# Graph attention on 16 row groups: the first group computes h W before its attention

## The chip, the cores and the metric

The kernel runs on one core of one Trainium2 chip. The metric is the device time of one execution in microseconds. The engines are named as in the profile: PE (TensorE), DVE (VectorE), ACT (ScalarE), POOL (GpSimd) and SP (SyncE, which issues transfers).

## What is computed

The input x is 128 graphs of 64 nodes with 512 features, in float32. One adjacency matrix serves all graphs. The reference, cut to what matters:

```python
h = jnp.maximum(_layernorm(x), 0.0)
# first layer, 4 heads, W: [4, 512, 512], a: [4, 1024]
Wh = einsum('bnf,hfo->bhno', h, W)
f1 = einsum('bhno,ho->bhn', Wh, a[:, :O]);  f2 = einsum('bhno,ho->bhn', Wh, a[:, O:])
e = f1[:, :, :, None] + f2[:, :, None, :]
e = where(e > 0, e, 0.01 * e);  e = where(adj > 0, e, -1e9)
attn = softmax(e, axis=-1)
h1 = elu(einsum('bhnm,bhmo->bhno', attn, Wh))      # heads side by side: 2048 features
# second layer: the same with one head and W_out: [2048, 512], then elu -> out
y = maximum(out @ w1 + b1, 0) @ w2 + b2 + out
x + layernorm(y) * gamma + beta
```

## The kernel before

The 8192 rows are 64 tiles of 128 rows (two graphs each). Four tiles form a group, and there are 16 groups. A group passes through norm and relu (`norm1`), scores and softmax, attention of the first layer (`attend1`), the projection by the four W (`project1`), the second layer (`project2`, `stage_e`) and the feed-forward part. The stages of neighbouring groups are interleaved: a main list of steps feeds TensorE, and a list of side steps is dealt out between them. The order on each engine is fixed when the program is built.

Attention and projection commute, because attention mixes rows and W mixes columns. The kernel uses this twice. First, it computes z = attention times h and then z W (`attend1`, `project1`). Each product is done in Strassen's way: seven products of quarter blocks ("pieces", four matmuls of 256 columns each) instead of eight, with sums of blocks formed on other engines. `weight_sums` forms the sums of the weight blocks on GpSimd and stores them to memory (`tc`); `piece` fetches blocks as they are needed. Second, the scores f1 and f2 come from h (W a), so the kernel folds a into W once at the start: `wa` holds W a for the four heads, and `project_f` and `scores1` make the scores of a group from it. `R`, `L` and `U` are what `project_f` makes.

The fold at the start is made in two ways. `spread_a` copies a row of a to all partitions with a matmul (tile `pab`), and `fold_dve` multiplies W by it and sums along the row on VectorE (tile `jk`, heads 0, 1 and 3). `fold_pe` transposes W on TensorE (tile `pwt`) and multiplies it by a (tile `pwa`, head 2).

So for group 0 nothing dense can start until W a is folded, the scores are made, the softmax is done and its weights are transposed (`transpose_weights`, tile `s1pt`). After that `attend1` (tile `pz`) and `project1` (tile `g_a`) run, and in between the scores of group 1 are made as side steps. `project2` of group 0 (tile `g_b`) follows.

PSUM has six banks for products (`bank`, tag "mm") and two more for small tiles (`aux`). W is loaded by ScalarE's queue at the very start, W_out, w1 and w2 later by GpSimd's queue (`fetch`, `more_sums`).

Of the kernel before, what the change touches and what calls it, by code (L numbers as in the profile page):

```python
# [22 lines left out]
def gat_preln_kernel(  # L23
# [27 lines left out]

    nc = tc.nc
# [25 lines left out]
    def bank(name):  # L78
        return ps.tile([P, 2, T], FP, tag="mm", name=name)

    def aux(shape, name):
        return ps.tile(shape, FP, tag="aux", name=name, bufs=2)
# [15 lines left out]
    X[0] = load(0)  # L98
    aj = const.tile([P, N], mybir.dt.int32, name="aj")
    for b in range(NB):  # L100
        nc.sync.dma_start(out=aj[ts(b, N), :], in_=adj)
    ar = wk.tile([2 * H, O], FP, tag="elu", name="ar", bufs=3)
    nc.sync.dma_start(out=ar, in_=a_heads.rearrange("h (r p) -> (h r) p", p=O))
    for t in range(1, G):
        X[t] = load(t)
    ah = wk.tile([2 * H * KC, P], FP, tag="elu", name="ah", bufs=3)
    nc.sync.dma_start(out=ah, in_=a_heads.rearrange("h (r p) -> (h r) p", p=P))
# [34 lines left out]
    homes = ("h11", "h22", "h12", "wh2", "out", "wh2", "out", "wh2", "out", "out")  # L142
    stages = ("ot", "rt", "out", "hS", "ot", "rt", "ot", "rt", "ot", "rt")
    MT, TC = {}, {}
    DIRECT = {}

    def fetch(m):
        MT[m] = big.tile([P, KC, O], FP, tag=homes[m], name=f"pw{m}")
        queue = nc.scalar if m < H else nc.gpsimd
        queue.dma_start(out=MT[m], in_=mats[m].rearrange("(k p) o -> p k o", p=P))  # L150

    def spread_a(m):

        ab = []
        for c in range(2):
            pb = bank(f"pab{m}_{c}").rearrange("p a b -> p (a b)")
            r = 2 * m + c
            nc.tensor.matmul(
                pb, ident[0:2 * H, r:r + 1].to_broadcast([2 * H, P]), ar, start=True, stop=True
            )  # L160
            ab.append(pb)
        return ab

    def turn_a():

        rows = H * 2 * KC
        pt = aux([P, rows], "pah")
        nc.tensor.transpose(pt, ah, ident[0:rows, 0:rows])
        aT = wk.tile([P, H, 2, KC], FP, tag="s1", name="aT")
        nc.scalar.copy(aT.rearrange("p h c o -> p (h c o)"), pt)  # L170
        return aT

    def fold_dve(m, ab):

        for k in range(KC):
            for c in range(2):
                junk = wk.tile([P, O], FP, tag="t", name=f"jk{c}_{m}_{k}")
                nc.vector.scalar_tensor_tensor(
                    junk, MT[m][:, k, :], 1.0, ab[c], ALU.mult, ALU.mult,
                    accum_out=wa[:, k, c * H + m:c * H + m + 1],  # L180
                )

    def fold_pe(m, aT):

        pw = aux([P, KC, 2], "pwa")
        for k in range(KC):
            pt = bank(f"pwt{m}_{k}").rearrange("p a b -> p (a b)").rearrange("p (o q) -> p o q", o=KC)
            for o in range(KC):
                nc.tensor.transpose(pt[:, o, :], MT[m][:, k, ts(o, P)], ident)
            wT = wk.tile([P, KC, P], FP, tag="elu", name=f"wT{m}_{k}", bufs=3)  # L190
            nc.scalar.copy(wT, pt)
            for o in range(KC):
                nc.tensor.matmul(
                    pw[:, k, :], wT[:, o, :], aT[:, m, :, o],
                    start=(k == 0 and o == 0), stop=(o == KC - 1), skip_group_check=True,
                )
        nc.scalar.copy(wa[:, :, m:m + H + 1:H], pw)

    def weight_sums(m, after=None):

        w = MT.pop(m)
        b11, b12 = w[:, 0:2, 0:Q], w[:, 0:2, Q:O]
        b21, b22 = w[:, 2:4, 0:Q], w[:, 2:4, Q:O]
        tag = stages[m]
        if tag[1] == "t":
            s = [big.tile([P, 2, 2, Q], FP, tag=f"{tag}{i}", name=f"pt{m}_{i}") for i in range(2)]
        else:
            both = big.tile([P, 2, 2, 2, Q], FP, tag=tag, name=f"pt{m}")
            s = [both[:, 0], both[:, 1]]
        free = [nc.gpsimd.tensor_tensor(s[0][:, 0], b12, b11, ALU.subtract)]  # L210
        nc.gpsimd.tensor_tensor(s[0][:, 1], b22, s[0][:, 0], ALU.subtract)
        free.append(nc.gpsimd.tensor_tensor(s[1][:, 0], b22, b12, ALU.subtract))
        for ins in free if after is not None else ():
            tc.add_manual_dep(
                ins.ins, after.ins.name,
                mybir.DependencyInfo(mybir.DependencyClass.Sync, mybir.DependencyReason.DATA),
                reason="the sums come behind it",
            )
        nc.gpsimd.tensor_tensor(s[1][:, 1], b21, s[0][:, 1], ALU.subtract)
        TC[m] = [dram.tile([P, 2, 2, Q], FP, name=f"tc{m}_{i}") for i in range(2)]  # L220
        for i in range(2):
            nc.gpsimd.dma_start(out=TC[m][i], in_=s[i])
        if m < 2:
            for p, i in ((5, 0), (6, 1), (7, 2), (4, 3)):
                DIRECT[m, p] = s[i // 2][:, i % 2]

    def piece(m, p):

        if (m, p) in DIRECT:
            return DIRECT.pop((m, p))  # L230
        w = ring.tile([P, 2, Q], FP, tag="w", name=f"w{m}_{p}")
        if p in (1, 2, 3):
            r, c = {1: (0, 0), 2: (1, 0), 3: (1, 1)}[p]
            src = mats[m][r * Q:(r + 1) * Q, c * Q:(c + 1) * Q].rearrange("(k p) o -> p k o", p=P)
        else:
            i = {5: 0, 6: 1, 7: 2, 4: 3}[p]
            src = TC[m][i // 2][:, i % 2]
        nc.sync.dma_start(out=w, in_=src)
        return w
# [100 lines left out]
    def norm_stats(src, tag, t):  # L340
# [4 lines left out]
        if tag == "n1" and t >= 2 * G:  # L345
            tc.add_manual_dep(
                ins.ins, LAST["pe"].ins.name,
                mybir.DependencyInfo(mybir.DependencyClass.Sync, mybir.DependencyReason.DATA),
                reason="x may come late: not in front of what is urgent",
            )  # L350
# [8 lines left out]
    def norm1(t):  # L359
# [7 lines left out]
        if t % G >= 2:  # L367
            HNS[t] = big.tile([P, T], FP, tag="hns", name=f"hns{t}", bufs=2)
            nc.gpsimd.tensor_tensor(HNS[t], HN[t][:, 0:T], HN[t][:, T:2 * T], ALU.add)
# [12 lines left out]
    def project_f(g):  # L382
# [15 lines left out]
        eng = nc.vector if g == 0 else nc.gpsimd  # L398
        eng.tensor_tensor(
# [167 lines left out]
    def flat(ap):  # L567
        return ap.rearrange("p a b -> p (a b)")

# [3 lines left out]
    def z_sums(g, h):  # L573
        z = ZB[g]
        ZSUM[h] = new_sums(f"z{g}_{h}")
        eng = nc.vector if (g, h) == (0, 0) else nc.gpsimd
        sums(eng, z["S1"][:, h], z["11"][:, h], z["12"][:, h], z["22"][:, h], *ZSUM[h])

    def project1(g, h):
# [3 lines left out]
        first = (g, h) == (0, 0)  # L583
        if h == 0:
            for b in ("11", "12", "S1", "22"):
                tag = "hS" if b == "S1" else "h" + b
                H1[b] = big.tile([P, H, 2, T], FP, tag=tag, name=f"h{b}_{g}")
# [3 lines left out]
        def post(what, a, b=None, to=None):  # L591
# [13 lines left out]
            post, (1, 2, 6, 5, 7, 3, 4) if first else (1, 5, 6, 2, 3, 7, 4),  # L605
# [9 lines left out]
        ]  # L615

# [180 lines left out]
    masks()  # L797
    for t in range(G):
        norm1(t)
    ab = {m: spread_a(m) for m in (0, 1)}  # L800
    aT = turn_a()
    fold_dve(0, ab[0])
    fold_dve(1, ab[1])
    fold_pe(2, aT)
    for t in range(G):
        transpose_h(t)
    fold_dve(3, spread_a(3))
    for m in range(H):
        weight_sums(m, LAST["nb"])
    project_f(0)  # L810
    scores1(0)
    for p in range(2):
        attn_weights(p)
    softmax_end = LAST["A"]
    transpose_weights(0)
    attn = attend1(0)
    for fn in attn[:2]:
        fn()
    head0 = project1(0, 0)
    for fn in head0[:2]:  # L820
        fn()
    transpose_weights(1)
    for fn in attn[2:]:
        fn()
    z_sums(0, 0)
# [14 lines left out]
    def more_sums(m):  # L840
        fetch(m)
        weight_sums(m, softmax_end)

    for t in range(G, 2 * G):
        prefetch(t)
    for g in range(NG):
        if g >= 1:
            side = stage_e(g - 1)
        else:
            side = sum(stage_a(1), [])  # L850
            for i, m in ((5, 4), (9, 5), (12, 6), (17, 7)):
                side.insert(i, lambda m=m: more_sums(m))
        done, n = 0, 6 * H
        for i in range(n):
            if i % 6 == 0:
                steps = head0 if (g, i) == (0, 0) else project1(g, i // 6)
            if (g, i // 2) != (0, 0):
                steps[i % 6]()
            while done * n < (i + 1) * len(side):
                side[done]()  # L860
                done += 1
        flush_late()
# [16 lines left out]
        if g == 0:  # L879
# [4 lines left out]
            run(project2(g), first + early + norms + scores + turns + [  # L884
# [39 lines left out]
```

## Time and profile before

| | us |
|---|---|
| median of 3 runs | 2320.62 (2318.3 to 2320.84) |
| span of the profiled run | 2318.7 |
| TensorE busy | 2279.8 (98%) |
| VectorE busy | 1272.2 (55%) |
| GpSimd busy | 1029.9 (44%) |
| ScalarE busy | 905.5 (39%) |

A line of a timeline gives the start, the length, the engine, the line of the code, the operation, the output and input tiles, their shapes and how many records were merged, and in brackets the idle time before them with what ended it. Busy time of TensorE is not work at its peak, since matmuls are pipelined. The profile also gives the clock that TensorE was granted, as a share of the full one.

### The profile page before, as it was taken

The numbers are of one execution on the slowest core, as the hardware profiler recorded it, in microseconds if no ns is written. First come the engines' busy times: TensorE is split into PE (matmuls) and PEld (weight loads), VectorE is DVE, ScalarE is ACT, GpSimd is POOL, SyncE is SP. The second block draws the span as 40 slices with busy tenths as digits, with TensorE's granted clock in tenths as the row PEclk, the third lists the DMA queues.
The fourth block names the chain that finished last, engine by engine and source line by source line (L and its number), as shares of the span: only waits on it lengthen the run. The fifth ranks groups of instructions, "written<-read, shape, count | busy, mean of one in ns | idle before, by whom it ended". The sixth has DMA issues, their size and how long they took to land. (4 is left out here: it accounts for less than half of the span.)

```text
span 2318.7 us, 33446 instructions
## 1 busy us (share of the span) xinstructions
PE 2279.8 (98%) x11933; PEld 1922.7 (83%) x11933; DVE 1272.2 (55%) x2210; ACT 905.5 (39%) x1623; POOL 1029.9 (44%) x917
## 2 busy tenths in 40 slices
PE   6999999999999999999999999999999999999997
PEld 4878888888888888888888888888888888888885
DVE  6635465555646555465555646555464654744427
ACT  2534425153352534425254252533525244251512
POOL 6664544425344352444425444253443525533324
PEclk8999999999999999999999999999999999999999
DMA  8545464554545445454454545445453454635543
GB/s 296 174 171 195 133 183 135 157 161 133 183 135 176 131 147 178 133 182 132 151 171 133 182 135 162 150 140 182 132 179 131 147 180 128 182 119 168 163 146 104
DMA packets 259571, 366.40 MB, mean 158 GB/s; under 512 B 24232, under 2 KB 147144, under 8 KB 259408
## 3 DMA queue, kind: packets, MB, share of 16 engines
q1 hardware_dynamic: 252784, 343.31, 47.3%
q0 software_dynamic: 4512, 16.78, 2.0%
q10 hardware_dynamic: 2112, 4.19, 0.5%
q8 instruction: 96, 1.57, 0.3%
q14 instruction: 67, 0.55, 0.1%
HBM read 336.92 MB, written 27.26 MB: 157 GB/s over the span
## 5 line engine op out<-in xcount | busy, mean ns | idle before, releaser
L322 PE MATMUL g_b<-w,h 128*128 128x256 f32 x2560 | 592.5, 379 | 0.0
L322 PEld LDWEIGHTS g_b<-w,h 128*128 128x128 f32 x2560 | 481.4, 190 | 63.7 <-issue 0.9
L307 PE MATMUL g_a<-z,w 128*128 128x256 f32 x1520 | 360.9, 380 | 0.7 <-DVE g_a L597 0.7
L307 PE MATMUL g_a<-zs_z,w 128*128 128x256 f32 x1504 | 350.9, 381 | 0.0
L307 PEld LDWEIGHTS g_a<-zs_z,w 128*128 128x128 f32 x1504 | 282.0, 190 | 60.8 <-issue 24.3
L307 PEld LDWEIGHTS g_a<-z,w 128*128 128x128 f32 x1520 | 287.2, 190 | 45.0 <-DVE g_a L597 6.1
L601 POOL TENSOR_TENSOR hS<-hS,h 128x512 f32<-128x512 f32 x64 | 83.1, 1299 | 354.8 <-DVE hS L565 354.8
L322 PE MATMUL g_b<-w,hS 128*128 128x256 f32 x1024 | 238.5, 379 | 0.0
L563 ACT ACTIVATE exc<-g_a 128x512 f32<-128x512 f32 x256 | 152.1, 594 | 179.0 <-DVE g_a L597 106.7
L565 DVE SCALAR_TENSOR_TENSOR h<-exc,g_a 128x512 f32<-128x512 f32 x192 | 131.7, 686 | 157.3 <-ACT exc L564 156.2
L322 PEld LDWEIGHTS g_b<-w,hS 128*128 128x128 f32 x1024 | 192.1, 190 | 25.8 <-issue 1.0
L564 ACT ACTIVATE exc<-exc 128x512 f32<-128x512 f32 x256 | 161.5, 631 | 7.0
L631 POOL TENSOR_TENSOR h<-h,h 128x512 f32<-128x512 f32 x64 | 86.8, 1364 | 135.3 <-PE g_b L322 135.3
L631 POOL TENSOR_TENSOR h<-hS,h 128x512 f32<-128x512 f32 x64 | 81.2, 1270 | 142.5 <-PE g_b L322 142.5
L481 ACT COPY at<-s1pt 128x512 f32<-128x512 f32 x64 | 34.7, 588 | 279.8 <-PE s1pt L479 279.8
L332 POOL TENSOR_TENSOR zs_z<-zS,z 128x512 f32<-128x512 f32 x63 | 89.0, 1414 | 122.6 <-PE g_a L307 118.6
L773 POOL TENSOR_TENSOR xr<-xr,bs 128x512 f32<-128x512 f32 x64 | 96.1, 1502 | 72.6 <-DMA xr<-in_x_dram 58.4
L307 PE MATMUL g_c<-ot,w 128*128 128x256 f32 x512 | 122.8, 383 | 1.4 <-DVE ot L735 1.4
L322 PE MATMUL g_d<-w,rt 128*128 128x256 f32 x512 | 121.5, 380 | 2.2 <-DVE o L765 1.5
L307 PE MATMUL g_a<-zS,w 128*128 128x256 f32 x496 | 117.2, 379 | 0.0
L655 DVE SCALAR_TENSOR_TENSOR jf<-wh,ao 128x512 f32<-128x512 f32 x128 | 99.0, 811 | 31.8 <-ACT wh L637 31.6
L333 POOL TENSOR_TENSOR zs_z<-z,zs_z 128x512 f32<-128x512 f32 x63 | 85.1, 1351 | 61.8 <-PE g_a L307 39.1
(159 smaller groups left out, 3485.8 us busy)
## 6 DMA issues: line engine op xcount, KB each, us to landing
w<-tc SPq DMA_DIRECT2D x632, 256.0 KB, 2.7
w<-in_L_gnn_W_heads_dram SPq DMA_DIRECT2D x192, 256.0 KB, 3.0
w<-in_L_gnn_W_out_dram SPq DMA_DIRECT2D x192, 256.0 KB, 2.7
w<-in_L_gnn_w_dram SPq DMA_DIRECT2D x96, 256.0 KB, 2.7
x<-in_x_dram SPq DMA_DIRECT2D x64, 256.0 KB, 3.8
xr<-in_x_dram SPq DMA_DIRECT2D x128, 128.0 KB, 2.7
out_dram<-o SPq DMA_DIRECT2D x128, 128.0 KB, 2.4
tc<-pt POOLq DMA_DIRECT2D x20, 512.0 KB, 4.2
```

Source lines behind the costliest of these rows:

```text
L307: LAST["pe"] = nc.tensor.matmul(bk[:, o, :], w[:, k, ts(o, P)], a[:, k, :], start=start and o == 0 and k == 0, stop=k == 1, skip_group_che ...
L322: LAST["pe"] = nc.tensor.matmul(bk[:, j, :], a[:, k, ts(j, P)], w[:, k, :], start=start and k == 0 and j == 0, stop=i == len(ms) - 1 and k ...
L332: eng.tensor_tensor(s2, s1, a11, ALU.subtract)
L333: eng.tensor_tensor(s4, a12, s2, ALU.subtract)
L481: nc.scalar.copy(AT[t].rearrange("p b h n -> p (b h) n"), pt)
L563: nc.scalar.activation(ex, src, AF.Relu, scale=-1.0)
L564: nc.scalar.activation(ex, ex, AF.Exp, scale=-1.0)
L565: nc.vector.scalar_tensor_tensor(dst, ex, -1.0, src, ALU.add, ALU.max)
L601: nc.gpsimd.tensor_tensor(dst, dst, H1["22"][:, h], ALU.add)
L631: nc.gpsimd.tensor_tensor(dst[:, h], x0[:, h], x1[:, h], ALU.subtract)
L655: nc.vector.scalar_tensor_tensor(junk, WH2[g][:, j], 1.0, ao[:, c, :], ALU.mult, ALU.mult, accum_out=f[:, c, j:j + 1],)
L773: nc.gpsimd.tensor_tensor(xr, xr, bs, ALU.add)
```

## The change

Group 0 is taken out of the scheme of the others. It computes h W directly (`head_w`, tile `hw`, 16 products of four matmuls of 512 columns, without Strassen), which needs only h and W. The scores of group 0 are read off these products: VectorE multiplies each by a spread row of a and sums along the row (tile `jw`, results in `f_0`). `scores0` spreads f2 with a matmul (tiles `dg` and `pe0`) and makes the softmax for two tiles at a time. `attend0` then applies the attention to h W, head by head, with matmuls of 64 columns (tile `pu`), and ends with the elu. `project2` of group 0 follows as before.

The fold of W a is needed from group 1 on. It is now made on VectorE alone, for all four heads (`fold`), between the steps of group 0. `spread_a` keeps a copy of the spread rows in SBUF (`asb`). The norms and transposes of group 1 move to the start; its scores, softmax and turns go into `project2` of group 0 as side steps, ahead of all others. The parts of W_out are fetched behind given products of h W.

The diff, cut to its core:

```diff
-    def fold_pe(m, aT):
...
-    def fold_dve(m, ab):
+    def fold(m, ab):
-        for k in range(KC):
-            for c in range(2):
+        for c in range(2):
+            for k in range(KC):
                 junk = wk.tile([P, O], FP, tag="t", name=f"jk{c}_{m}_{k}")
                 nc.vector.scalar_tensor_tensor(
                     junk, MT[m][:, k, :], 1.0, ab[c], ALU.mult, ALU.mult,
                     accum_out=wa[:, k, c * H + m:c * H + m + 1],
                 )
...
+    def head_w(m, j, asb):
+        pb = flat(bank(f"hw{m}_{j}"))
+        for k in range(KC):
+            LAST["pe"] = LAST["hw", m, j] = nc.tensor.matmul(
+                pb, HT[j][:, k, :], MT[m][:, k, :], start=k == 0, stop=k == KC - 1
+            )
+        nc.scalar.copy(flat(HW[j][:, m]), pb)
+        for c in range(2):
+            junk = wk.tile([P, O], FP, tag="t", name=f"jw{c}_{m}_{j}")
+            nc.vector.scalar_tensor_tensor(
+                junk, pb, 1.0, asb[c], ALU.mult, ALU.mult, accum_out=f_0[:, c, j, m:m + 1]
+            )
+    def scores0(p):
...
+        nc.vector.tensor_tensor(
+            dg, eye[:, None, :].to_broadcast([P, 2 * H, N]),
+            f2[:, :, None].to_broadcast([P, 2 * H, N]), ALU.mult,
+        )
+        pe = aux([P, 2 * H, N], f"pe0_{p}")
+        nc.tensor.matmul(
+            flat(pe), blkones.rearrange("p b n -> p (b n)"), flat(dg), start=True, stop=True,
+        )
+        A1[p] = softmax(pe, f1, 2 * H, "s1", p)
+    def attend0(h, r):
+        banks = [flat(bank(f"pu{h}_{r}_{b}")).rearrange("p (c j n) -> p c j n", c=KC, j=2) for b in range(NB)]
+        for j in range(2):
+            for c in range(KC):
+                for b in range(NB):
+                    rows = slice(b * N, (b + 1) * N)
+                    hw = HW[2 * r + j][rows, h, c // 2, (c % 2) * P:(c % 2 + 1) * P]
+                    nc.tensor.matmul(
+                        banks[b][:, c, j, :], hw, AT[2 * r + j][rows, b, h, :],
+                        start=True, stop=True, skip_group_check=True,
+                    )
...
-    ab = {m: spread_a(m) for m in (0, 1)}
-    aT = turn_a()
-    fold_dve(0, ab[0])
-    fold_dve(1, ab[1])
-    fold_pe(2, aT)
-    for t in range(G):
-        transpose_h(t)
-    fold_dve(3, spread_a(3))
...
-    project_f(0)
-    scores1(0)
...
+    block(0, range(G))
+    fold(0, spread[0][0])
+    weight_sums(0, LAST["nb"])
+    block(1, range(G))
+    fold(1, spread[1][0])
+    weight_sums(1, LAST["nb"])
+    norms[0]()
+    block(2, (0, 1))
+    fold(2, spread[2][0])
+    weight_sums(2, LAST["nb"])
+    norms[1]()
+    block(3, (0, 1))
+    scores0(0)
+    fold(3, spread[3][0])
+    more_sums(4)
+    block(2, (2, 3))
+    more_sums(5)
+    weight_sums(3, LAST["hw", 3, 1])
+    block(3, (2, 3))
+    scores0(1)
+    for m in (6, 7):
+        more_sums(m)
+    transpose_weights(0)
+    new_h1(0)
+    for fn in scores[:2]:
+        fn()
+    for h in range(H):
+        attend0(h, 0)
+    transpose_weights(1)
+    for h in range(H):
+        attend0(h, 1)
+    side1 = scores[2:] + turns
...
-            run(project2(g), first + early + norms + scores + turns + [
+            run(project2(g), side1 + first + early + norms + scores + turns + [
```

## The prediction

> **What bounds the kernel now.** First the slices of the page. TensorE is busy throughout except at the start, so whatever this change can win lies in the first 58 us and whatever comes later is a sum of matmuls.
>
> ```profile
> PE   6999999999999999999999999999999999999997
> PEclk8999999999999999999999999999999999999999
> ```
>
> The next view is TensorE's timeline of the start (start us, length, count in records; a float32 matmul is two records).
>
> ```profile
> 8.19 7.16 PE L158 MATMUL pab<-ar,ident 8*128 8x512 f32 x8 [8.19 <-DMA ar<-in_L_gnn_a_heads_dram]
> ...
> 40.37 1.99 PE L413 MATMUL s1pe<-R,L 64*64 64x256 f32 x16 [2.82 <-DVE n1ve L354]
> 47.74 1.94 PE L479 MATMUL s1pt<-ident,s1A 128*128 128x128 f32 x8 [5.38 <-DVE s1A L442]
> 49.61 6.22 PE L539 MATMUL pz<-at,hn 64*128 64x256 f32 x32
> ```
>
> Until 49.6 us TensorE only prepares scores, and waits for the softmax. Later in the same timeline:
>
> ```profile
> 75.24 1.89 PE L307 MATMUL g_a<-z,w 128*128 128x256 f32 x8
> 76.97 1.89 PE L307 MATMUL g_a<-zS,pt 128*128 128x256 f32 x8
> ...
> 115.68 1.89 PE L322 MATMUL g_b<-w,h 128*128 128x256 f32 x8
> 118.29 1.99 PE L307 MATMUL g_a<-z,w 128*128 128x256 f32 x8 [0.72 <-DVE g_a L597]
> ```
>
> One piece (four matmuls of 256 columns) takes 76.97 - 75.24 = 1.73 us. The second layer of group 0 starts at 115.7; with the last g_a piece and the wait ahead of it behind it (0.72 + 1.83), its start counts as 118.2. What follows is the same work in both kernels, so I compare this milestone.
>
> TensorE's clock in 2 us stretches (stretch, length, busy and count, clock, DMA share, GB/s):
>
> ```profile
> 40.00:42.00 2.00, 1.63 (x16) 0.57 0.92 264
> 48.00:50.00 2.00, 2.00 (x9) 0.50 0.96 367
> 52.00:54.00 2.00, 2.00 (x13) 0.51 0.33 127
> 54.00:56.00 2.00, 2.00 (x17) 1.00 0.00 0
> ```
>
> The clock is half until 54.0, 4.4 us after the pz matmuls begin. It was half before as well: pab advances 0.85 us per record of 512 columns, against 0.216 for 256 columns later, and transposes take 3.68/16 = 0.23 us at 17.5 us against 0.11 later. The 1.00 that the view prints before 36.9 is therefore a missing record, not a fast clock. At 40.3 the clock fell to half (0.57 in the first row) after TensorE had stood idle since 37.6.
>
> Last, weight loads of two tiles in small stretches of that timeline:
>
> ```profile
> 120.22 0.19 PEld L539 LDWEIGHTS pz<-at,hn 64*128 64x128 f32 x2 [0.33 <-issue]
> 120.22 0.30 PEld L539 LDWEIGHTS pz<-at,hn 64*128 64x128 f32 x4 [0.33 <-issue]
> ```
>
> Two loads for the two row halves run side by side in 0.19 us, and the next pair follows 0.11 us later. So 64-row loads overlap in pairs.
>
> And what VectorE, GpSimd and the queues pay for the operations that the change moves or repeats: VectorE's timeline, the answers on s2dg and on the transfers.
>
> ```profile
> 14.43 0.68 DVE L178 SCALAR_TENSOR_TENSOR jk<-pw,pab 128x512 f32<-128x512 f32 x1
> ...
> 15.04 0.68 DVE L178 SCALAR_TENSOR_TENSOR jk<-pw,pab 128x512 f32<-128x512 f32 x1
> ```
>
> ```profile
> L664 DVE TENSOR_TENSOR s2dg<-eye,f x16: 415/889/892, 194.1 to 2254.2; 128x256 f32<-128x256 f32 x16
> ```
>
> ```profile
> pw<-in_L_gnn_W_out_dram POOLq DMA_DIRECT2D x4, 1024.0 KB, 7.7
> ```
>
> One fold step starts 0.61 us after the one before; the diagonal for a score spread has a fast and a slow form; a 1 MB part of W_out lands 7.7 us after its issue.
>
> **What the Trainium skill says.** "TensorE: Matmul & The Clock Gate", Part 1 (The HAM clock gate): the array runs at half clock until it has been busy for a window of about 3.4 us, and falls back after one idle window. The trace agrees with both directions (54.0 and 40.3). It adds a condition: 7 us of pab on 8 rows and 20 us of transposes and 2-column matmuls did not raise the clock, so thin work hardly counts. Same page, LDWEIGHTS: the load's time goes by columns, not rows, and Part 3 says loads overlap where row groups differ; the pairs above agree. Part 1 also has ScalarE and VectorE as strict FIFO queues; the trace has nothing against it, and I use it twice.
>
> **The change, part by part** (times from the start, on the new order of instructions on each engine).
>
> *Start of the dense work.* hn0 and hn1 end at 15.1 (ScalarE loads its table at 12.25 in both kernels), hn2 and hn3 at 17.1; then two copies of a (0.6 each) and hT0: h W starts at 18.9. All W are there in time (the third landed at 17.5). Removed: the fold on TensorE (about 13 us of records between 17.5 and 30.6), hidden or not.
>
> *h W.* 16 products of 4 matmuls of 512 columns: 64 x 0.864 = 55.3 us at full clock (Strassen's 28 pieces took 48.4). Half clock for the first 4.4 us costs 2.2. Three further spreads of a, 2 x 0.87 each: 5.2. Transposes and a wait for hT2: 1.3. With 18.9 that is 82.9, call it 83. Banks come back early (the spread of head 1 needs only the reading of the first product), so no block waits for the folds.
>
> *VectorE beside it.* Each head has 8 jw and 8 jk, 9.8 us, under the 15.5 us of TensorE, but the order is one queue: 8 jk come after the last jw of a block, then the statistics of group 1 (4 x 1), then two softmaxes (8 operations of 0.69, about 5.5). From the end of head 1's product (52 us) VectorE has no gap: 36 us of work, until 88. Two waits lengthen this. hn4 stands on ScalarE ahead of the copy of head 2's second product, and its scale comes from GpSimd, behind the fetch of W_out's second part (issued after 45, median landing 7.7 us) and its four sums (1.27 each) and stores: about 62 against 60.5, so jw, and everything queued on VectorE behind it, moves by some 2 us; pe0_0 holds TensorE for as long. hn6 and hn7 do the same to the copies of head 2's later tiles: under 1 us. So h W ends at about 85.5, and dg1 (a 512-wide product; 0.7 to 1.7 us, from s2dg's 0.415 to 0.89 at half that size) ends at about 91.
>
> *The new gap.* TensorE stands from 85.5 to 91, longer than the idle stretch that lowered the clock at 40.3. I take half clock from there. Then pe0_1 1.7, s1pt pairs 2 x 0.95, four transposes of group 1 each behind a copy: the attention runs free from about 99.
>
> *Attention per head.* 8 rounds of 16 matmuls of 64 columns, 32 records, 16 pairs of loads. The trace shows no 64-column matmul on 64 rows. Bound below by pairs: 16 x 0.107 = 1.7 us at full clock, 3.4 at half. Bound above without overlap between loads: twice that. ScalarE needs 4 x 0.6 = 2.4 a round in the first half, 1.8 after; VectorE 1.5 to 2.1. Streaming fills only half of each pair's time (64 columns at 0.216 per 256 are 0.054, of 0.107), so I expect this not to raise the clock, as the transposes did not. I take 3.7 us a round at half clock: 29.6. The transposes in the middle with their copy add 2.2. Ends at 99 - 0.6 + 29.6 + 2.2 = 130.
>
> *Second layer.* Its first 4.4 us at half clock: 2.2 lost. Milestone 132.2 against 118.2: +14.
>
> *Moved.* Folded scores of group 1 (pf, s1pe, 16 s1pt) leave project1 and go into project2: 1.1 + 1.1 + 1.75 = 4.0 us of TensorE that the milestone no longer holds. Each softmax there (5.5 us) is followed by its transposes after three to four pieces of 1.73; GpSimd has R behind the hS sums. I estimate 2 us of waits (0 to 6).
>
> *Same answer, nothing:* other homes for W, the earlier a, the shorter list of direct pieces, R of group 0: all beside TensorE's h W. Groups 1 to 15 are untouched.
>
> Sum: 2318.7 + 14 + 4 + 2 = 2338.7 of span; times are 1.9 above spans (2320.63 for 2318.7): **2340**.
>
> **Rivals.**
> A. The clock stays high, or comes back in the attention. Then ScalarE paces it: 4 x 2.4 + 4 x 1.8 and copies, 18 us; the chain before it shrinks by 4, and the 2.2 go. Milestone about 114 to 117; with 4 + 2 and the 1.9: 2322 to 2325. For it: pz on 64 rows did raise the clock. Against: pz streams without pause, and the gap comes first.
> B. Faster than before: A and no gap, since VectorE is quicker or waits overlap. Milestone 83 + 5 of scores + 18 = 106, give or take 2; with 4 + 1 and the 1.9: 2312 to 2315. For it: 30 us less idle start. Against: VectorE's 36 us, counted from a measured step.
> C. Loads do not overlap at 64 columns, or TensorE starts a load only after the previous stream: 5 to 7 us a round, 8 x 1.3 to 8 x 3.3 more: 2350 to 2366. For it: no row measures it; against: the pairs.
>
> **How the numbers follow.** Main case (half clock in the attention, 2326 to 2350 with the bounds of gap, dg and waits): 0.57. A: 0.18. B: 0.12. C: 0.13. Within 0.2% is 2316 to 2325.3: A, less its upper edge. Faster 0.12, same 0.17, slower 0.71. The range leaves out most of B and the upper end of C: 2317 to 2356.
>
> **What would show it.** In the profile after: hw records from about 19 us, clock 1.00 from about 23; h W ending at 83 to 86; a wait of pe0 on VectorE's dg of 4 to 6 us; clock 0.50 in the pu stage, pairs of pu every 0.22 us or so; g_b from 130. Wrong if pu runs at 1.00, if the gap is missing, or if g_b starts before 118.

## The result, and the profile after

The changed kernel takes 2352.08 us (median of 4 runs, 2350.49 to 2357.86), the kernel before 2320.3 in the same runs: a ratio of 1.0143, with a 95% interval of 1.0125 to 1.0161. It is slower, by 31.8 us. The profiled execution is the slowest of the four (2357.86, a span of 2355.8), so the trace holds some 6 us more than the median run; in which stage they lie is not known.

Two lines of the slices on the page: TensorE starts dense work sooner, and the clock has a dip in the second and third slice that before did not have.

```profile
PE   7899999999999999999999999999999999999997
PEclk9789999999999999999999999999999999999999
```

TensorE's timeline of the first group:

```profile
18.75 9.71 PE L592 MATMUL hw<-pw,hT 128*128 128x512 f32 x16 [2.19 <-ACT hT L351]
...
75.52 9.60 PE L592 MATMUL hw<-pw,hT 128*128 128x512 f32 x22
93.41 2.04 PE L611 MATMUL pe<-dg,blkones 128*128 128x512 f32 x2 [8.29 <-DVE dg L606]
95.25 2.11 PE L449 MATMUL s1pt<-ident,s1A 128*128 128x128 f32 x8
...
103.12 13.49 PE L624 MATMUL pu<-at,hw 64*128 64x64 f32 x122
116.54 1.97 PE L449 MATMUL s1pt<-ident,s1A 128*128 128x128 f32 x8
118.88 2.04 PE L624 MATMUL pu<-at,hwS 64*128 64x64 f32 x16 [0.38 <-ACT at L451]
...
132.80 3.78 PE L297 MATMUL g_b<-w,h 128*128 128x256 f32 x8
```

h W starts at 18.75. In before the attention (`pz`) starts at 49.61, so the new way starts 30.9 us sooner. The second layer, though, starts at 132.80 in place of 118.2. The 114 us between are 66.4 of h W (to 85.1), 8.3 of waiting for dg, 3.7 of scores and transposes (93.4 to 97.1) and 35.7 of attention. Before needs 68.6 us from 49.61 to 118.2. The attention of group 0 comes in eight rounds, one for each head and pair of tiles; a round is 16 matmuls of 64 columns, 32 records.

The clock in 2 us stretches (busy time and count, clock, DMA share, GB/s) shows where it falls:

```profile
88.00:90.00 2.00, 0.00 (x0) 0.70 0.97 307
90.00:92.00 2.00, 0.00 (x0) 0.50 0.95 301
```

It falls in the wait for dg, and stays at 0.50 until 136.6, through all of the attention. In the second layer and in the next projection come waits that before did not have:

```profile
150.07 1.89 PE L449 MATMUL s1pt<-ident,s1A 128*128 128x128 f32 x8 [2.10 <-DVE s1A L412]
...
186.82 2.30 PE L349 MATMUL pth<-ident,hn 128*128 128x128 f32 x8 [4.57 <-ACT hn L337]
...
239.70 3.78 PE L282 MATMUL g_a<-zs_z,w 128*128 128x256 f32 x8 [2.92 <-ACT t_a L248]
```

The first is for the softmax of group 1 (`s1A`), the second for the norms of group 2 (`hn`), the third for a copied sum in the projection (`t_a`). In each of the three the clock falls some 2.2 us after TensorE has stopped, and is at half from 150.2 to 153.7, 184.4 to 191.2 and 239 to 245.8. From the second layer of group 1 on (234.40 before, 271.58 after) the two kernels need the same: 2084.3 and 2084.2 us. So all of the loss lies ahead of that point, in three stages. The table has every kernel of this study (start of g_b of group 0, of g_a of group 1, of g_b of group 1, and the span, in us, of the profiled execution):

| kernel | g_b, group 0 | g_a, group 1 | g_b, group 1 | span |
|---|---|---|---|---|
| before | 115.7 (counts as 118.2) | 184.5 | 234.4 | 2318.7 |
| after | 132.8 | 215.5 | 271.6 | 2355.8 |
| e1 | 130.7 | 213.9 | 268.7 | 2352.3 |
| e2 | 135.4 | 221.4 | 276.1 | 2359.5 |
| e3 | 130.4 | 211.2 | 267.5 | 2351.5 |
| e4 | 132.9 | 215.7 | 271.9 | 2355.9 |
| e5 | 128.9 | 209.0 | 265.9 | 2349.1 |
| e6 | 132.9 | 210.0 | 263.3 | 2347.4 |
| e7 | 133.3 | 217.7 | 269.0 | 2352.1 |
| b1 | 128.6 | 204.2 | 257.4 | 2341.0 |
| b2 | 123.6 | 197.6 | 250.6 | 2334.3 |
| b3 | 124.1 | 203.3 | 254.6 | 2338.5 |
| f2 | 119.9 (counts as 122.5) | 188.7 | 238.7 | 2322.2 |
| f3 | 116.4 (counts as 118.9) | 185.8 | 235.8 | 2319.3 |

The first stage loses 14.6 us (132.8 - 118.2), the second 16.4 (82.7 against 68.8 - 2.5 for the late piece of g_a), the third 6.2 (56.1 against 49.9). Together 37.2, the difference of the two spans being 37.1. The first stage's loss is told by what TensorE did in it:

| us | before, 49.61 to 118.2 | after, 18.75 to 132.80 | e5, 18.75 to 128.86 |
|---|---|---|---|
| waits | 1.4 | 9.0 | 2.8 |
| matmuls without use | | | 22.4 |
| all other instructions | 67.3 | 105.1 | 84.9 |

The last row of e5 is the work of after at a clock that was held up (see e5 below). So the new way is 84.9 - 67.3 = 17.6 us more work for TensorE here, half clock lengthens it by another 20.2, and the waits add 7.6. Together that is 45.4 us, against the 30.9 of the earlier start.

### The profile page after: what moved, and what is told of

Read it like the earlier page. It is cut to its first block, busy times and chain, and to the rows that moved or that the text cites. A ratio compares the mean times of both kernels' runs of the same rounds, so it can differ in the third digit from the quotient of the medians.

```text
span 2355.8 us, 33480 instructions
## 1 busy us (share of the span) xinstructions
PE 2306.5 (98%) x11940; PEld 1919.3 (81%) x11940; DVE 1299.6 (55%) x2289; ACT 902.5 (38%) x1615; POOL 1017.7 (43%) x906
## 5 line engine op out<-in xcount | busy, mean ns | idle before, releaser
L282 PE MATMUL g_a<-z,w 128*128 128x256 f32 x1440 | 343.0, 381 | 0.0
L282 PE MATMUL g_a<-zs_z,w 128*128 128x256 f32 x1440 | 338.0, 383 | 2.9 <-ACT t_a L248 2.9
L282 PEld LDWEIGHTS g_a<-zs_z,w 128*128 128x128 f32 x1440 | 271.0, 191 | 62.9 <-issue 24.3
L282 PEld LDWEIGHTS g_a<-z,w 128*128 128x128 f32 x1440 | 273.4, 191 | 41.9 <-DVE g_a L565 4.9
L569 POOL TENSOR_TENSOR hS<-hS,h 128x512 f32<-128x512 f32 x60 | 78.1, 1301 | 354.3 <-DVE hS L535 354.3
L533 ACT ACTIVATE exc<-g_a 128x512 f32<-128x512 f32 x240 | 142.6, 594 | 163.5 <-DVE g_a L565 95.6
L535 DVE SCALAR_TENSOR_TENSOR h<-exc,g_a 128x512 f32<-128x512 f32 x180 | 123.6, 687 | 141.8 <-ACT exc L534 141.2
L534 ACT ACTIVATE exc<-exc 128x512 f32<-128x512 f32 x240 | 151.4, 631 | 6.7
L297 PEld LDWEIGHTS g_d<-w,rt 128*128 128x128 f32 x512 | 97.0, 190 | 17.0 <-DVE o L793 2.7
L282 PEld LDWEIGHTS g_c<-ot,w 128*128 128x128 f32 x512 | 94.9, 190 | 19.3 <-issue 5.0
```

The costliest lines, as they stand in the source:

```text
L282: LAST["pe"] = nc.tensor.matmul(bk[:, o, :], w[:, k, ts(o, P)], a[:, k, :], start=start and o == 0 and k == 0, stop=k == 1, skip_group_che ...
L297: LAST["pe"] = nc.tensor.matmul(bk[:, j, :], a[:, k, ts(j, P)], w[:, k, :], start=start and k == 0 and j == 0, stop=i == len(ms) - 1 and k ...
L533: nc.scalar.activation(ex, src, AF.Relu, scale=-1.0)
L534: nc.scalar.activation(ex, ex, AF.Exp, scale=-1.0)
L535: nc.vector.scalar_tensor_tensor(dst, ex, -1.0, src, ALU.add, ALU.max)
L569: nc.gpsimd.tensor_tensor(dst, dst, H1["22"][:, h], ALU.add)
```

## The experiments

**The theories.** T: the loss is half clock in the attention, caused by the wait for dg on VectorE, plus the waits that the moved steps meet in the second layer. R1: h W without Strassen and attention in 64 columns are more work, and do not win at any clock. R2: GpSimd's sums beside VectorE's softmax make the wait for dg, and that alone is the loss. Matmuls "without use" below write to a bank that nobody reads; they only keep TensorE busy.

**e1, the wait for dg filled,** with matmuls of 512 columns without use.

```diff
     block(3, (2, 3))
+    filler(9)
     scores0(1)
...
     transpose_weights(0)
+    filler(1)
     new_h1(0)
     for fn in scores[:2]:
         fn()
+        filler(1)
```

> Twelve matmuls of 512 columns without use are put where TensorE waits: nine behind the last product of h W, ahead of pe0_1, one behind the four transposes of group 0, one behind each of the first two transposes of group 1. The waits on VectorE stay as they are. Theory T (the half clock in the attention is what the change loses, the gap on VectorE is what causes it): the clock stays at 1.00 from 24 to at least 97; if the attention of 64 columns holds it, a round of it takes 2.4 us (ScalarE) in place of 3.4, the second layer starts at 115 to 119 in place of 132.8, and the time is 2334 to 2340. If the attention itself lets the clock fall although nothing stood before it, the second layer starts at 127 to 132 and the time is 2347 to 2352. Rival R1 (h W without Strassen and the attention of 64 columns are simply more work): the time stays at 2350 to 2354 also with the clock at 1.00, since a round doesn't get shorter.

Measured: 2352.69 us (2349.61 to 2354.36), ratio 1.0141 [1.0125, 1.0156]: no gain. TensorE's timeline of e1:

```profile
92.96 1.10 PE L611 MATMUL pe<-dg,blkones 128*128 128x512 f32 x2 [0.52 <-DVE dg L606]
...
100.35 0.66 PE L349 MATMUL pth<-ident,hn 128*128 128x128 f32 x4 [1.53 <-ACT hT L351]
100.94 13.21 PE L624 MATMUL pu<-at,hw 64*128 64x64 f32 x128
```

The clock now stayed at 1.00 until 101.8, and then fell all the same, after a wait of 1.5 us on a copy. 128 records took 13.2 us, as in after. Held until the attention began, the clock was not held in it. T's first part does not stand as it was put.

**e2, the folds of heads 2 and 3 moved into the attention.**

```diff
-    fold(2, spread[2][0])
...
-    fold(3, spread[3][0])
...
         attend0(h, 0)
+        fold(2, spread[2][1], (2 * h, 2 * h + 1))
...
         attend0(h, 1)
+        fold(3, spread[3][1], (2 * h, 2 * h + 1))
```

> The folds of heads 2 and 3 (16 operations jk of 0.61 us, 9.8 us of VectorE) leave the stage of h W and are dealt out over the eight rounds of attention, two a round, reading the copies of the spread rows in SBUF. Theory T: the wait of pe0_1 on VectorE's dg falls from 8.3 us to under 1, the clock stays at 1.00 into the attention, the second layer starts at 112 to 120, the time is 2328 to 2340. If the clock falls in the attention all the same, the start comes at 122 to 128 and the time is 2340 to 2347. Rival R1: the gap goes (some 6 to 8 us), the rounds stay at 3.4 us, time 2343 to 2346. Rival R2 (GpSimd's sums stretch VectorE's operations in SBUF, and that alone makes the gap): the gap stays at 4 us or more, since s1e still takes 2.4 and 3.3 us.

The run also swaps the places in SBUF of two parts of W. Measured: 2360.05 us (2355.52 to 2361.65), 8 us above after by the medians. 9.8 us of VectorE went out of the way, but the wait for dg only fell from 8.29 to 6.00; of what was expected only R2's part came, a wait of 4 us or more. VectorE's timeline of e2:

```profile
91.82 1.75 DVE L184 SCALAR_TENSOR_TENSOR jk<-pw,asb 128x512 f32<-128x512 f32 x1
...
98.52 4.88 DVE L184 SCALAR_TENSOR_TENSOR jk<-pw,asb 128x512 f32<-128x512 f32 x1
```

The same step takes 0.68 us when it reads the spread row from PSUM (pab). Read from the copy in SBUF (asb), beside GpSimd's sums, it takes up to 4.88, and 0.68 again at 105.36, when GpSimd computes nothing. What e2 saved at one place it paid at another, and with the second softmax queued behind.

**e3, GpSimd's sums behind the first softmax.**

```diff
     scores0(0)
+    A0 = LAST["A"]
     fold(3, spread[3][0])
-    more_sums(4)
...
-    more_sums(5)
-    weight_sums(3, LAST["hw", 3, 1])
...
+    weight_sums(4, A0)
+    weight_sums(5, A0)
+    weight_sums(3, A0)
```

> GpSimd's sums of the blocks of W_out's first two parts and of W of head 3 move behind the first softmax of group 0; nothing else changes. R2 (GpSimd beside VectorE stretches the softmax's operations in SBUF, 2.43 and 3.34 us in place of 0.69): these operations go back to about 0.7, the wait of pe0_1 falls from 8.3 to 3.5 to 5 us. Theory T adds that the clock falls all the same, as 3.5 us is enough for it, and the time goes down by the gap alone: 2346 to 2349. If R2 alone made the loss, the clock stays at 1.00 and the time is 2335 to 2340.

Measured: 2351.53 us (2350.2 to 2353.31), ratio 1.0135 [1.0118, 1.0152]. The first softmax on VectorE, in after:

```profile
76.93 2.43 DVE L400 TENSOR_TENSOR s1e<-s1e,negm 128x512 f32<-128x512 f32 x1
79.28 0.68 DVE L182 SCALAR_TENSOR_TENSOR jk<-pw,pab 128x512 f32<-128x512 f32 x1
...
82.30 3.34 DVE L404 TENSOR_TENSOR s1e<-s1e,s1mx 128x512 f32<-128x512 f32 x1
```

and in e3:

```profile
76.58 0.69 DVE L400 TENSOR_TENSOR s1e<-s1e,negm 128x512 f32<-128x512 f32 x1
...
80.20 0.69 DVE L404 TENSOR_TENSOR s1e<-s1e,s1mx 128x512 f32<-128x512 f32 x1
```

So 4.4 us of the wait for dg are GpSimd's doing: it fell from 8.29 to 3.88. The rest is VectorE's own queue. R2 is right about half of that wait, and wrong about the loss, since the time hardly moved. TensorE's timeline of e3 tells why:

```profile
88.66 2.04 PE L611 MATMUL pe<-dg,blkones 128*128 128x512 f32 x2 [3.88 <-DVE dg L606]
...
95.67 5.34 PE L624 MATMUL pu<-at,hw 64*128 64x64 f32 x90
103.44 4.31 PE L624 MATMUL pu<-at,hw 64*128 64x64 f32 x32 [2.43 <-DVE h L638]
```

Here the clock came back to 1.00 at 91.6, and 90 records took 5.34 us, 1.9 us a round. Then TensorE waited for h, the elu on VectorE, which stood behind the second softmax; that softmax now had the sums beside it (one of its operations took 4.82). The clock fell 0.8 us into that wait and stayed at half for the other five rounds. Three rounds fill the six banks of PSUM, so their pace says nothing of how fast ScalarE and VectorE would empty them.

**e4, norms of group 2 ahead of the sums of z, in the list of steps.**

```diff
-            run(project2(g), side1 + first + early + norms + scores + turns + [
+            run(project2(g), side1 + first + norms + early + scores + turns + [
```

> In the second layer of group 0 the norms of group 2 are put ahead of the sums of z, on all engines. Theory T (part of the loss lies in waits that the moved steps meet there, GpSimd's queue above all): the wait of 4.57 us on hn at 186.8 and the half clock from 184 to 191 go or shrink to under 1 us, and the time goes down by 3 to 6: 2346 to 2349. If the transposes only wait for another thing in that place, the time stays within 1.5 us of 2352.

Measured: 2352.35 us (2351.47 to 2357.71), no difference. On GpSimd's queue the six sums of z still stood ahead of n1rs, the scale that the norms need: an order of steps in the program is not an order on an engine. This run says nothing on T.

**e5, the clock held throughout.** As e1, with one such matmul of 512 columns behind each round as well.

```diff
     for h in range(H):
         attend0(h, 0)
+        filler(2 if h == 2 else 1)
     transpose_weights(1)
+    filler(1)
     for h in range(H):
         attend0(h, 1)
+        filler(1)
```

> The matmuls without use of e1, and further ones: one more behind each of the two transposes of group 1, and one of 512 columns (0.86 us at full clock) behind each round of the attention (two behind the third round, one behind the transposes in the middle). Theory T2 (64-column rounds hold the clock only as long as nothing interrupts them; in e1 the wait of the third round on VectorE, whose queue has the second softmax ahead of the elu, let it fall): the clock stays at 1.00 from 24 us to beyond the start of the second layer, a round takes 2.5 to 2.8 us with its filler, the second layer starts at 122 to 127, the time is 2341 to 2347. Rival R3 (rounds of 64 columns can't be held at full clock even with 0.86 us of dense work in each): the clock falls near 102 as in e1, the fillers take twice as long, and the time is 2358 or more. R1 (the work itself is more, whatever the clock): T2's times still stand well above 2320, so that even at full clock the whole cannot win; under 2330 would speak against R1.

Measured: 2352.25 us (2351.05 to 2353.27), ratio 1.0137 [1.0122, 1.0152]. TensorE's timeline of e5:

```profile
104.90 2.00 PE L624 MATMUL pu<-at,hw 64*128 64x64 f32 x32
106.84 1.12 PE L869 MATMUL fill<-pw,hT 128*128 128x512 f32 x2
107.89 2.00 PE L624 MATMUL pu<-at,hw 64*128 64x64 f32 x32
```

and a stretch of its clock:

```profile
104.00:108.00 4.00, 4.00 (x38) 1.00 0.63 152
```

R3, the idea that rounds of 64 columns cannot be held at full clock, falls: the clock stays at 1.00 from 22 to 144 us, and a round takes 1.93 us in place of 3.41. But each was given its 1.05 us of dense work, and the second layer starts at 128.9, only 4 us earlier; the time was expected at 2341 to 2347 and did not fall. The full clock gave back 20.2 us of the first stage, 8 x (3.41 - 1.93) = 12 of them in the rounds, the rest in h W and in the scores and transposes. But the 15 matmuls outside the wait for dg cost 14.5 us, and the other waits grew by 1.6. Take the 14.5 away on paper and the second layer would start at 114, with the wait for dg still whole (8.4, filled): with the 4.0 us of work that moved behind this point, about even with before. Take that wait and the 2.3 us of the others away as well, and it would start at 103.7, some 10 us ahead of before with the moved work counted. So R1 is right that there is more work, but TensorE's own sum (17.6 and 4.0 us more, a start 30.9 us sooner) speaks against its second half, that the new way cannot win at any clock. That the other engines could deliver in time for this is not shown.

**e6, the norms of group 2 among the attention of group 1,** as in all later groups, and the first sums of z behind them by a dependence.

```diff
+        else:
+            first[4:4] = norms[:1]
+            first += norms[1:]
...
+        if g == 1 and h < 2:
+            behind(first, LAST["nb"], "the norms first")
```

> Only the second layer of group 0 is changed: the norms of group 2 follow the attention of group 1's second and last tile, as in all later groups, and the first two sums of z on GpSimd wait for the norms (e4 had moved the norms in the list of steps, but on GpSimd's queue they stayed behind six sums). Theory T: the wait of 4.57 us on hn goes to under 1, the half clock of 184 to 191 goes with it, the time falls by 4 to 7: 2345 to 2348. If it is something else that the transposes wait for: 2350 to 2353.

Measured: 2345.8 us (2342.68 to 2349.23), ratio 1.0105 [1.0088, 1.0122]: 6.3 us less than after, as expected. TensorE's timeline of e6:

```profile
181.34 1.04 PE L350 MATMUL pth<-ident,hn 128*128 128x128 f32 x8
...
192.63 1.09 PE L384 MATMUL s1pe<-R,L 64*64 64x256 f32 x16 [1.78 <-POOL R L370]
...
234.44 1.99 PE L282 MATMUL g_a<-zs_z,w 128*128 128x256 f32 x8 [3.08 <-ACT t_a L248]
```

The wait of 4.57 and its half clock are gone; the sums of z, now later, hold up R for 1.78. The projection of group 1 starts 5.4 us sooner than in after (210.0 against 215.5), so T's second part is shown for this place. Part of the gain was luck, though: the wait on t_a is as long as in after (3.08 and 2.92), but here no half clock follows it, and this stage is 2.9 us shorter. The last section shows why one such wait costs more than another.

Why the norms were late is seen on GpSimd, in before and in after:

```profile
138.99 2.50 POOL L332 TENSOR_TENSOR zs_z<-zS,z 128x512 f32<-128x512 f32 x2 [0.56 <-DVE zS L553]
...
175.19 2.50 POOL L307 TENSOR_TENSOR zs_z<-zS,z 128x512 f32<-128x512 f32 x2 [0.62 <-DVE zS L523]
```

In both, the norms stand behind six sums of z. But in before these begin 23 us after the start of the second layer (115.7), in after 42 us, since the steps put ahead of them push them back.

**e7, loads and sums of w1 and w2 earlier, on top of e6.** In after, VectorE has this line in the next projection:

```profile
233.10 5.32 DVE L401 SCALAR_TENSOR_TENSOR s2e<-s2e 128x256 f32<-128x256 f32 x1
```

and GpSimd these:

```profile
233.20 1.28 POOL L308 TENSOR_TENSOR zs_z<-z,zs_z 128x512 f32<-128x512 f32 x1
...
236.87 1.25 POOL L307 TENSOR_TENSOR zs_z<-zS,z 128x512 f32<-128x512 f32 x1
```

The sums of z stood behind the load and the sums of w2 and met the softmax of the second layer, an operation of which waited until four operations of GpSimd (three of them sums of z) were through; behind it on VectorE's queue stood the sum that t_a, for which TensorE waited 2.92 us, is copied from.

```diff
-            run(project2(g), side1 + first + early + scores + turns + [
-                load_rows, lambda: sums_late(M1), lambda: sums_late(M2)
-            ])
+            run(project2(g), side1 + [lambda: sums_late(M1)] + first + [lambda: sums_late(M2)]
+                + early + scores + turns + [load_rows])
...
-    side1 = scores[2:] + turns
+    side1 = scores[2:] + [nothing] * 2 + turns
```

> As e6, and in the second layer of group 0 the loads and GpSimd sums of w1 and w2 come right behind the softmax of group 1 and the attention of group 1, in place of the end of the stage; two empty steps more stand ahead of the transposes of group 1's weights. Theory T: in after the sums of z for heads 1 and 2 stood behind those of w2, which waited for their load, ran beside the softmax of the second layer and stretched one of its operations to 5.3 us; so the wait of 2.9 us on t_a and the half clock behind it (239 to 246) go, with the wait of 2.1 us on s1A at 150: the time falls by 6 to 9 from e6, to 2337 to 2340. If the stretching comes from elsewhere: 2343 to 2347.

Measured: 2350.44 us (2347.51 to 2353.92), ratio 1.0127 [1.011, 1.0144]: by the medians 4.6 above e6, though the two intervals overlap. Both waits that it was aimed at went as expected: none on t_a, s1A at most 0.65 us. A new one took their place. On GpSimd the sums of w2 wait for their load, and the norms stand behind them:

```profile
172.83 1.26 POOL L194 TENSOR_TENSOR pt<-pw 128x512 f32<-128x512 f32 x1 [8.65 <-DMA pw<-in_L_gnn_w_dram]
...
180.82 0.26 POOL L336 TENSOR_SCALAR n1nb<-n1mv,n1rs 128x1 f32<-128x1 f32 x1
```

On ScalarE the norm stands ahead of the copy that frees TensorE's bank:

```profile
181.12 1.69 ACT L338 ACTIVATE hn<-x,n1nb,n1rs 128x512 f32<-128x512 f32 x2 [13.11 <-POOL n1nb L336]
182.71 0.57 ACT L522 COPY zS<-pzS 128x512 f32<-128x512 f32 x1
```

and TensorE waits for that copy:

```profile
183.33 2.08 PE L510 MATMUL pzS<-at,hns 64*128 64x256 f32 x8 [8.44 <-ACT zS L522]
```

Read from the end: TensorE waits for a copy, the copy for a norm, the norm for sums of w2 and these for a transfer of 1 MB. Neither the attention nor the norm needs w2.

**b1, b2, b3, another order.** h W of tiles 0 and 1 first; then the first softmax while TensorE makes h W of tiles 2 and 3, with the first rounds between its products; GpSimd's sums of parts 3, 5, 6 and 7 of W behind the first softmax; pf of group 1 in the wait for the second; the second layer as in e6. b2 adds a few matmuls without use and puts one of the first four rounds into the wait for the second softmax; b3 is b2 with the moves of e7.

```diff
+    block(0, (2, 3))
+    norms[1]()
+    block(1, (2, 3))
...
+    attend0(0, 0)
+    block(2, (2,))
+    attend0(1, 0)
+    block(2, (3,))
+    block(3, (2,))
+    attend0(2, 0)
+    block(3, (3,))
+    scores0(1)
```

> Another order of group 0: h W of tiles 0 and 1 for all heads first, then the first softmax while TensorE makes h W of tiles 2 and 3, with the first four rounds of attention between its products; GpSimd's sums wait until the first softmax is done; group 1 has its transposes and pf in the wait for the second softmax; the second layer as in e6. Theory T2: the wait for dg falls to under 4, the clock stays at 1.00 until about 95, the first four rounds cost 1.7 to 1.9 us each, the second layer starts at 112 to 118 if the clock falls at the second softmax, and the time is 2318 to 2328. R1 (more work in any order): 2335 or more.

> As b1, with one of the first four rounds behind pe0_1, and with matmuls without use in the wait for the second softmax (512 columns each, three) and of 256 columns behind the transposes and each of the last four rounds. T2: the clock stays at 1.00 throughout from 24, the second layer starts at 109 to 114, the time is 2313 to 2321. If the fillers cost what they save: within 2 us of b1.

> b2 with the same two moves as e7. T: 6 to 9 us less than b2's 2336: 2327 to 2331. R1 says that it still stays above 2320, since TensorE is busy at full clock from 19 us to the start of the second layer at 123; a time under 2319 would refute R1.

Measured: b1 2343.02 (2342.44 to 2345.36), b2 2336.25 (2335.58 to 2337.51), b3 2341.52 (2340.37 to 2344.95); ratios 1.0099 [1.0084, 1.0114], 1.0069 [1.0054, 1.0084], 1.0095 [1.008, 1.011]. All three lie above what T expected, by 15, 15 and 10.5 us over the upper ends; R1's part of b1's and b3's expectations, 2335 or more and above 2320, came true. b3 has e7's new wait, of 8.62. b2 is the best version with h W first. TensorE's timeline of b2:

```profile
58.09 2.05 PE L615 MATMUL pe<-dg,blkones 128*128 128x512 f32 x2 [3.32 <-DVE dg L610]
...
102.17 1.13 PE L615 MATMUL pe<-dg,blkones 128*128 128x512 f32 x2 [2.75 <-DVE dg L610]
...
123.60 1.89 PE L298 MATMUL g_b<-w,h 128*128 128x256 f32 x8
```

Its clock is at 1.00 except from 57 to 64 and 135 to 139 us, and the mean is 0.996, with 0.995 in before. Still the second layer starts 5.4 us later than in before and takes 7.7 us longer. In the 104.8 us of the first stage there are 6.1 us of the two waits for dg, 2.2 of other waits, 5.5 of matmuls without use, 1.3 of pf, which after has later, and about 2.7 of half clock behind the first wait. Without the two waits and the matmuls without use the second layer would start at 112, without all of these at 106, against 118.2 in before. This fits the sum from e5, and is worked out like it and not run.

**f2 and f3, the start of before with the clock held.** The kernel before with its own order, the spread of a for head 3 at the start, and matmuls without use in the first 48 us. f3 has fewer of them, and the statistics of group 1 behind the softmax.

```diff
-    ab = {m: spread_a(m) for m in (0, 1)}
+    for m in (0, 1, 3):
+        ab[m] = spread_a(m)
...
-    fold_dve(3, spread_a(3))
+    fold_dve(3, ab[3])
```

> The kernel before, with its own way of starting, but with TensorE's clock held up by matmuls without use in the first 48 us (four ahead of the first spread of a, two behind each pair, one ahead of each group of transposes, three and five in the two waits), and with the spread of a for head 3 moved to the start, so that VectorE's fold doesn't wait for it behind the transposes of W. If the idle start of before costs its time by the clock and by that wait: the clock is at 1.00 from about 10 us to the end, the fold on VectorE ends at 29 in place of 37.6, the first dense g_a starts at 43 to 48 in place of 55.8, the time is 2308 to 2314. If W's loads or the softmax bound the start all the same: 2316 to 2321.

> f2 with fewer matmuls without use (one behind the second and third spread, none ahead of two of the transposes of h, two in place of three ahead of s1pe), and with the statistics of group 1 on VectorE behind the second softmax of group 0. In f2 these statistics stood ahead of U on VectorE's queue, waiting 10.55 us for GpSimd, so that R came 6 us late and TensorE idled 5.0 us and fell to half clock. If that was the cause: R is done at 37 to 38, s1pe starts at 37 to 39 (f2 45.3, before 40.4), the first g_a at 49 to 52 (f2 60.1, before 55.8), the time is 2313 to 2318, less than both kernels. If another wait takes its place: 2319 to 2325.

Measured: f2 2325.66 (2324.31 to 2326.16, 11 runs), ratio 1.0023 [1.0014, 1.0032]; f3 2321.13 (2319.98 to 2325.29, 13 runs), 1.0009 [1.0001, 1.0018]. The fold on VectorE ended at 28.5 and 28.8 in place of 37.6, and TensorE gained nothing from it. In f2 VectorE stood for GpSimd, with U behind:

```profile
43.45 0.41 DVE L369 BATCH_NORM_AGGREGATE n1mv<-n1st 128x2 f32<-128x6 f32 x2 [10.55 <-POOL n1nb L381]
```

In f3 that is gone, but R ran beside GpSimd's sums of W:

```profile
37.85 2.92 DVE L418 TENSOR_TENSOR R<-U,headrow 128x512 f32<-128x512 f32 x1
```

f3's first g_a starts at 55.06, behind a wait of 1.66 us, before's at 55.80; another wait of 1.62 us follows. No version of this study beats the kernel before.

## Why the prediction was right, and where it was off

The direction was right and the time lies in the range, 12 us above the predicted point. The main mechanism, a wait on VectorE and half clock through the attention, came as predicted. But its case was to end at 2350; the measured time lies above that, where only rival C was expected, whose mechanism did not come. So that the range holds it is in part luck. The profiled span is 17.1 us above the predicted one, and 14.7 of these are the last term of the sum, the waits in the second layer. By its steps:

- **The rest is the same in both kernels:** right, to 0.1 us (2084.3 and 2084.2).
- **h W from 18.9 to 85.5:** measured 18.75 to 85.1. The end is right, but partly by luck: TensorE did not wait at pe0_0 for hn4 at all. What stands in place of these 2 us are pe0_0 itself (0.86 us, which the sum had left out), 0.5 for the spreads of a (1.91 each), 0.5 for the products at full clock (3.49 each, 3.46 counted) and 0.4 for half clock, which lasted until 23.9.
- **The gap, 85.5 to 91:** it came, and was 8.29 us. The mis-sized term is "two softmaxes (8 operations of 0.69, about 5.5)": two of the operations took 2.43 and 3.34, 4.4 us more (e3). The wait is only 2.8 us longer than predicted, so some 2 us were saved elsewhere; it had counted about as much for hn4, which did not come. The Trainium skill's page "SBUF — State Buffer", Who interferes with whom, says that a VectorE instruction with two inputs in SBUF shuts out, or is shut out by, a GpSimd instruction that reads SBUF. The traces agree, down to jk: 0.68 from PSUM, up to 4.88 from SBUF (e2). The prediction had not used it.
- **Half clock from the gap through the attention:** right (0.50 from 88.8 to 136.6). e1 and e3 show that closing or shortening the gap alone does not save the clock: beside rounds of 64 columns it falls at the next wait (1.53 us in e1, 0.8 us into a wait in e3).
- **A round, 3.7 us at half clock:** 3.41 measured. The loads go in pairs, so rival C falls. At full clock a round is 1.9 us (e3, e5). Rival A had put ScalarE's 2.4 as the limit for the first four; no run tests that, since e3 has three such rounds in a row and e5 has 2.98 us from one to the next.
- **The second layer from 130:** it started at 132.80. The gap ended at 93.4 in place of 91, which is 2.4 of the 2.8 us; the way from there took 39.4, with 39 predicted. Its slow start cost 1.9, 2.2 predicted.
- **Moved, 4.0 us:** agrees: pf 1.10, s1pe 1.09, and about 1.8 for s1pt.
- **Waits of 2 us (0 to 6):** this is the step that failed. In the profiled run it is 37.2 - 14.6 - 1.9 - 4.0 = 16.7, far outside its own bounds. The prediction thought only of the softmax and its transposes (2.10 and 0.65), and of R (0.24). It left out the norms of group 2, late behind sums of z that the longer list of steps had pushed back (4.57, shown by e6), and the softmax of the second layer beside the late sums of z (2.92; e7 removes it, but moves other steps with it). And it counted no half clock behind waits, which adds some 7 us to the 9.6 of the three. It had taken one idle window of about 3.4 us as what lets the clock fall, and its own case, at 40.3, was a stop of 2.8; here 2.1 us were enough.
- **Rival B, faster:** e5 and b2 speak against it. Even with the clock up the second layer starts at 128.9 and 123.6, where B had 106. B's figure itself is close to what TensorE's work alone comes to, 103.7 from e5; what B lacked are the waits, and what it costs to hold the clock.

Not settled: whether VectorE, ScalarE and GpSimd could keep pace with TensorE's sum. A version without the waits was not reached, so it is neither shown that h W first must lose nor that it can win. The fold on VectorE alone was not tried by itself in the kernel before. Nor was e6 tried with the sums of w1 alone moved, which would tell the two parts of e7 apart.

## What to carry to other kernels

Work that starts earlier is not yet a gain: count what the new way costs at the clock that it will have, and expect attention in 64 columns to run at half clock unless dense matmuls stand between its rounds (e5). When steps move into a stage that was full, write down for each in-order queue what now stands ahead of what. The norms behind the sums of z (after), the elu behind a softmax (e3) and the copy behind a norm (e7) needed nothing from what they stood behind. And keep two-input operations on SBUF of VectorE's critical chain away from GpSimd's sums, or give them an operand in PSUM.

## What the runs showed of the hardware

- A VectorE operation with two inputs in SBUF does not only wait for the GpSimd operation under way. s2e took 5.32 us while four GpSimd operations of some 1.27 us ran back to back (233.2 to 238.1 in after). Operations with one operand in PSUM, and TENSOR_REDUCE, kept their 0.68 beside them (jk from pab at 81.70 and s1mx at 81.10 in after).
- Rounds of 64-column matmuls held the full clock from 95.7 to 101 in e3 while they ran without a break, yet 27 us of them did not raise it in after. One matmul of 512 columns to a round (1.05 of 2.98 us) held it in e5.
- In each of the 14 traces the recorded changes of the clock lie whole multiples of 3.41 us apart (in after at 88.81, 136.60, 150.25, 153.67, 184.39 and so on). So a wait costs by how much of it falls into one such interval. The three waits of after put 2.10, 2.14 and 2.22 us of idle time into one, and the clock fell at its end. The 3.08 us of e6 were split into 1.25 and 1.82, and it stayed. Near 1.9 both occur (1.91 us stayed in b1, 1.86 fell in f3). With rounds of 64 columns in the rest of the interval less was enough: 1.53 us in e1, 0.83 in e3.
- The loads of the attention's matmuls (64 rows by 128 columns of h W) go in pairs, one pair in 0.213 us at half clock (16 records in 1.71 us).
